# An attention and a convolution layer over eight images: the last 64 gated channels contracted in two row halves, one contraction moved into a parameter chain, and a weight loaded ahead of the last input band

## The chip, the cores and the metric

The kernel runs on one core of a Trainium2 chip. The time is the device time of one execution in microseconds (us). Three executions of the kernel before took 3504.19, 3505.67 and 3510.26 us; the median is 3505.67. In profile lines PE is TensorE (PEld its weight loads), DVE is VectorE, ACT is ScalarE, POOL is GpSimd and SP is SyncE, which mainly issues DMAs. L738 means line 738 of the kernel before.

## The reference

Eight float32 images of 384 channels and 64x64 pixels pass through two residual layers, each behind a group normalisation over 32 groups. The first is linear attention with six heads; the second a patchwise Fourier filter, a depthwise 3x3 convolution and a gated output product. In outline:

```
t = group_norm(x)
q, k, v = Wq t + bq, Wk t + bk, Wv t + bv      # rotary positions on q and k; then elu + 1
x = x + Wfc (q (k^T v) / (q . sum k)) + bfc
t = w_in group_norm(x)                          # 384 -> 384 channels
t = irfft2(rfft2(8x8 patches of t) * fft_filter)
t = depthwise_3x3(t, w_dw)
x1, x2 = t[:, :192], t[:, 192:]
x = x + w_out (gelu(x1) * x2)                   # 192 -> 384 channels
```

The change concerns the last line: the product with w_out contracts over 192 channels, one and a half times the 128 rows of the array.

## The kernel before, in words

An image has 4096 tokens (pixels), worked on in 8 bands of 512; its 384 channels are three tiles of 128 (index m or t). Every matmul is float32, and each one in the code appears as two instructions in the profile. PSUM is used as eight banks of 128x512 that `ps_tile` hands out in turn, so a matmul that takes a bank first waits until the bank's last reader has finished.

For each image b there are two stages. The query stage, `queries` (from L810), projects the queries (`pq`, L525), normalises them and projects the attention output (`pf`, L604), adding it into x. In its first band it also runs the gate of the previous image's last band, and in its third band (L848) it calls `output`, the contraction of that band. Then comes the parameter chain of the second normalisation, `norm_chain(b, 1, ...)` (L922 to L929): group sums and their redistribution as very small matmuls (`ps_m`, `ps_mc`, `ps_v`, `ps_r`) with small DVE steps in between (L289 to L313). For images 0 to 6 the first key projections of the next image fill the chain; for image 7 there is no next image, and nothing fills it.

The layer-1 stage is the loop at L933 to L968, nine steps for eight bands. A step j holds: `expand_filter` (`pi` L622, with ScalarE copies to `ht` L629, and the forward transform `pd` L636 in 64x64 tiles of the array, then the filter on DVE, L644); `back_transform` (`pb` L653, copied by ScalarE into a ring of rows, L660, whose borders GpSimd copies, L669); `first_taps` (L700, ScalarE); key projections of the next image (`pk` L430, bias on DVE into `kc` L433, rotary products L413, L421 and L437, then L337) and their accumulation (`acc` L445); the contraction of band j-2 (`contract`, L738); and, at the end, `depthwise_gate` of band j-1. That gives 7 contractions in a layer-1 stage and one in the next image's query stage. Image 7's own layer-1 stage (L980 to L996) has no next image beside it; it holds all of that image's 8 contractions, and its last two bands take the third channel tile's taps on TensorE.

`depthwise_gate` is 24 tap instructions of DVE (L714; the first of the nine taps is made by ScalarE in `first_taps`), then `gate_taps` (L717 to L723): channels 0 to 127 of x1 go through a gelu in ScalarE (L720) and are multiplied by x2 on DVE (L722); the other 64 channels of x1, on partitions 0 to 63 of the third tile, go through a 64x512 gelu (L721) into partitions 64 to 127 of the second half of `gated`, where they are multiplied by x2 (L723). Partitions 0 to 63 of that second half stay zero (L260), as do the matching rows of `w_out` (L247).

`contract` then needs two matmuls for each output tile, both with 128 rows and N=512; in the second, half of the rows are zeros:

```
for m in range(CT):
    p_ = ps_tile(f"pw_{b}_{j}_{m}")
    for s in range(2):
        nc.tensor.matmul(p_, w_out[:, s, m * P : (m + 1) * P], g[:, s, :], start=(s == 0), stop=(s == 1))
```

DVE adds each tile to x (L744). For image 7's bands 0 to 6 ScalarE copies it to `y` instead (L742), a GpSimd DMA accumulates y into x (L749), and SP sends x out (L751); the last band goes out in three DMAs.

At the start SP's queue loads x's eight bands (the first in three DMAs, L145; the others L147), then the key weight wk (L224). ScalarE's queue loads group masks and the key bias `bk_bc`. DVE computes statistics of each band as it lands (L157). In `layer0_chain` (L754) the group sums of wk (`sum_weight`, `pg_wk` L343) are issued after the fourth step of the parameter chain.

The order of instructions on each engine is fixed when the program is built; at run time an engine takes its own in that order and waits on semaphores.

## Time and profile before

| | |
|---|---|
| median of three runs | 3505.67 us |
| the profiled execution | 3504.77 us, of which the span from first to last instruction is 3503.0 |
| mean granted TensorE clock | 0.994 |
| PE / DVE / ACT / POOL busy | 98% / 83% / 52% / 4% |
| contraction matmuls (L738) | 768 instructions, 343.0 us busy |
| taps on DVE (L714) | 1520 instructions, 1054.8 us |
| x adds on DVE (L744) | 171 instructions, 115.9 us |
| gate products on DVE (L722; L723 of 64x512) | 64, 43.6 us; 62, 42.7 us |
| gelus on ACT (L720; L721 of 64x512) | 39.9 us; 39.0 us |

A group's line names source line, engine, operation, the tile written and those read, shapes and count; then its busy time and the mean of one in ns, the idle time of the engine ahead of it and what ended most of that. Consecutive matmuls overlap: a matmul of N=512 is listed with 596 ns, but from the start of one to that of the next takes about 430. The cost of a stretch of matmuls is therefore read from start to start. In a row of a table of stages come the window, its length, the busy time and count of PE, PEld, DVE, ACT and POOL, the granted clock, the DMA share and GB/s. In a timeline a row is a stretch of alike instructions: start, length, engine, line, operation, tiles, count, and in brackets the idle time ahead of it and its releaser.

### The profile page before, as it was taken

How to read it: one execution, taken by the hardware profiler on the slowest of the kernel's cores; microseconds unless marked ns; L12 is line 12 of the kernel's file. 1: busy time of each engine (PE TensorE's matmuls, PEld its weight loads, DVE VectorE, ACT ScalarE, POOL GpSimd, SP SyncE). 2: the span in 40 equal slices, each digit the busy share in tenths (PEclk: the TensorE clock that was granted, in tenths of full speed). 3: DMA queues.
4: the chain of work that ended last, by engine and by line, in shares of the span. 5: the costliest groups of instructions: out<-in, count | busy, mean ns of one | idle time of the engine just before them, and what ended most of it. 6: DMA issues, size and time to landing. Idle time of an engine off the chain costs nothing.

```text
span 3503.0 us, 38501 instructions
## 1 busy us (share of the span) xinstructions
PE 3438.7 (98%) x14384; PEld 1872.3 (53%) x14384; DVE 2894.7 (83%) x4499; ACT 1805.7 (52%) x3242; POOL 128.3 (4%) x305
## 2 busy tenths in 40 slices
PE   8999999999999999999999999999999999999998
PEld 5545565455554556545565455644555446554454
DVE  7586998868988699886998869987799877998688
ACT  4445563456544565445553555635655354534553
POOL 0000000000000000000000000000000000000011
PEclk9999999999999999999999999999999999999999
DMA  6321233212332122321223212232123211222013
GB/s 214 110 70 52 73 101 113 76 52 73 109 109 84 49 81 90 117 79 46 99 73 129 67 45 100 94 108 67 46 99 116 97 56 34 75 80 88 15 45 90
DMA packets 124641, 290.76 MB, mean 83 GB/s; under 512 B 26101, under 2 KB 36518, under 8 KB 116262
## 3 DMA queue, kind: packets, MB, share of 16 engines
q1 hardware_dynamic: 123110, 282.39, 23.9%
q0 software_dynamic: 1008, 5.51, 0.8%
q8 instruction: 113, 1.85, 0.2%
q14 instruction: 74, 0.61, 0.1%
q10 hardware_dynamic: 336, 0.41, 0.0%
HBM read 232.44 MB, written 50.33 MB: 81 GB/s over the span
## 4 chain that ended last, share of the span: by engine, by line
PE 79%; DVE 12%; issue 4%; ACT 3%; POOL 1%; DMA 1%; ACTq 0%; POOLq 0%
PE pq L525 15%; PE pf L604 15%; PE acc L445 12%; PE pk L430 11%; PE pi L622 8%; DVE dw L714 7%; PE pw L738 7%; PE pb L653 3%; PE pd L636 2%; PE px L396 1%; PE pn L563 1%; DVE kc L437 1%; ACT ring L660 1%; POOL ring L669 1%; DVE x L744 1%
## 5 line engine op out<-in xcount | busy, mean ns | idle before, releaser
L714 DVE SCALAR_TENSOR_TENSOR dw<-ring,w_dw,dw 128x512 f32<-128x512 f32 x1520 | 1054.8, 747 | 118.5 <-ACT dw L700 96.1
L430 PE MATMUL pk<-wk,x 128*128 128x384 f32 x1536 | 542.8, 493 | 0.1
L525 PE MATMUL pq<-x,wq 128*128 128x512 f32 x1152 | 520.2, 599 | 0.7
L604 PE MATMUL pf<-qc,mt 128*128 128x512 f32 x1152 | 513.7, 599 | 0.0
L622 PE MATMUL pi<-w_in,hf 128*128 128x384 f32 x1536 | 509.8, 489 | 2.2 <-ACT hf L330 1.4
L445 PE MATMUL acc<-xk,kc 128*128 128x385 f32 x1488 | 502.4, 490 | 9.0 <-DVE kc L337 9.0
L445 PEld LDWEIGHTS acc<-xk,kc 128*128 128x128 f32 x1488 | 279.9, 190 | 227.1 <-issue 46.5
L622 PEld LDWEIGHTS pi<-w_in,hf 128*128 128x128 f32 x1536 | 290.6, 191 | 200.6 <-issue 5.5
L430 PEld LDWEIGHTS pk<-wk,x 128*128 128x128 f32 x1536 | 279.2, 192 | 177.2 <-issue 21.5
L525 PEld LDWEIGHTS pq<-x,wq 128*128 128x128 f32 x1152 | 212.8, 190 | 252.3 <-issue 234.6
L604 PEld LDWEIGHTS pf<-qc,mt 128*128 128x128 f32 x1152 | 213.4, 190 | 249.6 <-issue 232.5
L738 PE MATMUL pw<-gated,w_out 128*128 128x512 f32 x768 | 343.0, 596 | 0.6 <-DVE gated L722 0.6
L397 ACT COPY xk<-px 128x384 f32<-128x384 f32 x248 | 116.4, 478 | 343.1 <-PE px L396 342.2
L629 ACT COPY ht<-pi 128x384 f32<-128x384 f32 x256 | 121.5, 475 | 234.0 <-PE pi L622 233.4
L608 DVE SCALAR_TENSOR_TENSOR x<-pf,bfc,x 128x512 f32<-128x512 f32 x192 | 141.1, 743 | 107.5 <-PE pf L604 106.8
L738 PEld LDWEIGHTS pw<-gated,w_out 128*128 128x128 f32 x768 | 141.5, 191 | 159.0 <-issue 141.9
L653 PE MATMUL pb<-idft,tf 128*128 128x128 f32 x1536 | 188.9, 278 | 11.6 <-DVE tf L644 11.6
L653 PEld LDWEIGHTS pb<-idft,tf 128*128 128x128 f32 x1536 | 181.7, 193 | 31.2 <-DVE tf L644 20.7
L433 DVE TENSOR_TENSOR kc<-pk,kbias 128x384 f32<-128x384 f32 x256 | 141.1, 551 | 68.3 <-PE pk L430 67.0
L660 ACT COPY ring<-pb 128x512 f32<-128x512 f32 x192 | 109.7, 580 | 158.1 <-PE pb L653 157.4
L335 ACT ACTIVATE qs<-qc 128x1536 f32<-128x1536 f32 x64 | 95.0, 1484 | 170.5 <-DVE qc L554 160.5
L335 ACT ACTIVATE ks<-kc 128x1536 f32<-128x1536 f32 x64 | 95.0, 1485 | 136.1 <-DVE kc L437 124.4
(153 smaller groups left out, 4032.2 us busy)
## 6 DMA issues: line engine op xcount, KB each, us to landing
tq<-in_tq SPq DMA_DIRECT2D x64, 1024.0 KB, 4.8
tk<-in_tk SPq DMA_DIRECT2D x64, 768.0 KB, 4.3
x<-in_x SPq DMA_DIRECT2D x63, 768.0 KB, 4.6
out_dram<-x SPq DMA_DIRECT2D x63, 768.0 KB, 3.3
xs<-in_x SPq DMA_DIRECT2D x56, 768.0 KB, 5.1
x<-y POOLq DMA_DIRECT2D x7, 768.0 KB, 5.7
wk<-in_wk SPq DMA_DIRECT2D x8, 576.0 KB, 4.0
wv<-in_wv SPq DMA_DIRECT2D x8, 576.0 KB, 6.1
```

The costliest lines, as they stand in the source:

```text
L335: nc.scalar.activation(e, x_, AF.Relu, scale=-1.0)
L430: nc.tensor.matmul(pk[:, :C], tokens(t), wks[:, t, :], start=(t == 0), stop=(t == CT - 1))
L433: nc.vector.tensor_add(kc[:, i, :], pk[:, :C], bias)
L445: nc.tensor.matmul(acc[m][:, : C + 1], kf[:, i, m * P : (m + 1) * P], xk[:, i, :], start=(j == 0 and i == 0), stop=(j == NBAND - 1 and i = ...
L525: nc.tensor.matmul(p_, wqs[:, t, m * P : (m + 1) * P], xt[b, j][:, t, :], start=(t == 0), stop=(t == CT - 1),)
L604: nc.tensor.matmul(p_, mt[:, t, m * P : (m + 1) * P], q[:, t, :], start=(t == 0), stop=(t == CT - 1))
L608: nc.vector.scalar_tensor_tensor(xm, p_, bfc[:, m : m + 1], xm, ALU.add, ALU.add)
L622: nc.tensor.matmul(p_[:, :C], h[:, t, i * P : (i + 1) * P], w_in[:, t, :], start=(t == 0), stop=(t == CT - 1),)
L653: nc.tensor.matmul(patches[:, k // 2, k % 2], tf[:, k, m * P : (m + 1) * P], idft.rearrange("p (u n) -> p u n", u=2), start=True, stop=True,)
L660: nc.scalar.copy(t[:, m, 1:9, 1 : W + 1].rearrange("p r (b c) -> p r b c", c=8), p_.rearrange("p (b r c) -> p r b c", b=8, r=8),)
L714: nc.vector.scalar_tensor_tensor(acc[:, m], src, wd, acc[:, m], ALU.mult, ALU.add)
L738: nc.tensor.matmul(p_, w_out[:, s, m * P : (m + 1) * P], g[:, s, :], start=(s == 0), stop=(s == 1))
```

## The change

The contraction becomes a generator, `contraction`. The output is split into two token halves of 256 (h). The products of the first 128 channels come first, for all three output tiles and both halves (N=256). Then the last 64 channels: rows 0 to 63 of the array hold the first 256 tokens, rows 64 to 127 the last 256, as two row tiles of 64x128 with N=256, so that no row holds zeros. Four PSUM banks are held instead of three, by pairs of output tiles (0 and 1; 2) and halves. The gate writes the halves in two 64x256 gelus, one of them to a new tile `gelu2`, and two 64x256 products. The adds become two of 128x(2x256) and two of 128x256, all behind the half products; ScalarE's copies for image 7 likewise, and the last band's output goes in four DMAs.

Image 6's last contraction leaves image 7's query stage and is spread over the steps of image 7's parameter chain. At the start, x's first band is one DMA, wk is loaded ahead of x's last band, `bk_bc` moves from ScalarE's queue to SP's behind that band, and `sum_weight(wk)` is issued ahead of the parameter chain. The last 64 rows of w_out are loaded twice and the two zero fills go.

```diff
--- before.py
+++ after.py
@@ -19,6 +19,7 @@
 N = H * W
 NBAND = 8
 BT = N // NBAND
+HT = BT // 2
 NH = 6
 HD = 64
 NG = 32
@@ -140,11 +141,7 @@
         if b >= nb:
             return
         t = xp.tile([P, CT, BT], F32, tag="x", name=f"x_{b}_{j}")
-        if b == j == 0:
-            for m in range(CT):
-                nc.sync.dma_start(t[:, m], x_in[b][:, m, j * BT : (j + 1) * BT])
-        else:
-            nc.sync.dma_start(t, x_in[b][:, :, j * BT : (j + 1) * BT])
+        nc.sync.dma_start(t, x_in[b][:, :, j * BT : (j + 1) * BT])
         xt[b, j] = t
     stats, moments = {}, {}
@@ -207,7 +204,7 @@
     group_w = {}
-    for j in range(NBAND):
+    for j in range(NBAND - 1):
         load_x(0, j)
     k_runs = ((0, 0, C),)
@@ -239,12 +236,12 @@
     )
     ident = groups[:, 2 * CT * NG :]
     of_group = const_tile([NG, C], "of_group", a["of_group"])
-    bk_bc = const_tile([P, C], "bk_bc", a["bk"].partition_broadcast(P))
     first_wk = load_weight(0, "wk", k_runs)
+    load_x(0, NBAND - 1)
+    bk_bc = const_tile([P, C], "bk_bc", a["bk"].partition_broadcast(P), nc.sync)
     scale = HD ** -0.5
     halves = (slice(0, 64), slice(64, P))
     w_out = const.tile([P, 2, C], F32, tag="w_out", name="w_out")
-    nc.gpsimd.memset(w_out[0:64, 1, :], 0.0)
     kvt_bd = const.tile([P, CT, P], F32, tag="kvt_bd", name="kvt_bd")
@@ -256,8 +253,8 @@
     for i in range(2):
         ring.append(const.tile([P, CT, 10, W + 2], F32, tag=f"ring{i}", name=f"ring{i}"))
-    gated = const.tile([P, 2, BT], F32, tag="gated", name="gated")
-    nc.gpsimd.memset(gated[0:64, 1, :], 0.0)
+    gated = const.tile([P, BT + HT], F32, tag="gated", name="gated")
+    gelu2 = const.tile([P, HT], F32, tag="gelu2", name="gelu2")
     def norm_chain(b, layer, params):
@@ -717,38 +714,65 @@
         g = gated
         af = dw.pop((b, j)).rearrange("p t r w -> p t (r w)")
         last = dw_pe.pop((b, j)) if on_array(b, j) else af[:, 2, :]
-        nc.scalar.activation(g[:, 0, :], af[:, 0, :], AF.Gelu)
-        nc.scalar.activation(g[64:P, 1, :], last[0:64, :], AF.Gelu)
-        nc.vector.tensor_mul(g[:, 0, :], g[:, 0, :], af[:, 1, :])
-        nc.vector.tensor_mul(g[64:P, 1, :], g[64:P, 1, :], last[64:P, :])
+        nc.scalar.activation(g[:, :BT], af[:, 0, :], AF.Gelu)
+        nc.vector.tensor_mul(g[:, :BT], g[:, :BT], af[:, 1, :])
+        for h, gelu in enumerate((gelu2[64:P, :], g[64:P, BT:])):
+            of = slice(h * HT, (h + 1) * HT)
+            nc.scalar.activation(gelu, last[0:64, of], AF.Gelu)
+            nc.vector.tensor_mul(g[halves[h], BT:], gelu, last[64:P, of])
     def depthwise_gate(b, j):
         taps(b, j)
         gate_taps(b, j)
-    def contract(b, j):
-        g = gated
+    def contraction(b, j):
         x_ = xt.pop((b, j))
         adding = b == nb - 1 and j < NBAND - 1
+        pairs = ((0, 2), (2, 3))
+        ps = [[ps_tile(f"pw_{b}_{j}_{m0}_{h}").rearrange("p (m n) -> p m n", m=2) for h in range(2)] for m0, _ in pairs]
+        for (m0, m1), p_ in zip(pairs, ps):
+            for m in range(m0, m1):
+                for h in range(2):
+                    nc.tensor.matmul(
+                        p_[h][:, m - m0, :],
+                        w_out[:, 0, m * P : (m + 1) * P],
+                        gated[:, h * HT : (h + 1) * HT],
+                        start=(m == m0),
+                        stop=False,
+                    )
+            yield
+        for (m0, m1), p_ in zip(pairs, ps):
+            for m in range(m0, m1):
+                for h, half in enumerate(halves):
+                    nc.tensor.matmul(
+                        p_[h][:, m - m0, :],
+                        w_out[half, 1, m * P : (m + 1) * P],
+                        gated[half, BT:],
+                        start=False,
+                        stop=(m == m1 - 1),
+                    )
+            yield
         y = w_tile([P, CT, BT], f"y_{b}_{j}") if adding else None
         to = x_out[b][:, :, j * BT : (j + 1) * BT]
-        for m in range(CT):
-            p_ = ps_tile(f"pw_{b}_{j}_{m}")
-            for s in range(2):
-                nc.tensor.matmul(
-                    p_, w_out[:, s, m * P : (m + 1) * P], g[:, s, :], start=(s == 0), stop=(s == 1)
-                )
-            if adding:
-                nc.scalar.copy(y[:, m, :], p_)
-            else:
-                nc.vector.tensor_add(x_[:, m, :], p_, x_[:, m, :])
-                if b == nb - 1:
-                    nc.sync.dma_start(to[:, m], x_[:, m, :])
+        for (m0, m1), p_ in zip(pairs, ps):
+            for h in range(2):
+                of = (slice(None), slice(m0, m1), slice(h * HT, (h + 1) * HT))
+                if adding:
+                    nc.scalar.copy(y[of], p_[h][:, : m1 - m0, :])
+                else:
+                    nc.vector.tensor_add(x_[of], p_[h][:, : m1 - m0, :], x_[of])
+                    if b == nb - 1:
+                        nc.sync.dma_start(to[of], x_[of])
         if adding:
             nc.gpsimd.dma_start(out=x_, in_=y, accum_op=ALU.add)
         if adding or b < nb - 1:
             nc.sync.dma_start(to, x_)
+    def contract(b, j):
+        run(contraction(b, j))
     def layer0_chain(b, prepared):
@@ -756,10 +780,9 @@
             return
         wk = load_weight(b, "wk", k_runs) if b else first_wk
         params = []
-        for i, _ in enumerate(norm_chain(b, 0, params)):
-            if b == 0 and i == 3:
-                sum_weight(wk, "wk")
-            yield
+        if b == 0:
+            sum_weight(wk, "wk")
+        yield from norm_chain(b, 0, params)
         scale_weight(wk, params)
         yield
         prepared += params, wk, k_bias(b, params)
@@ -845,7 +868,7 @@
                 run(output_)
                 if j < NBAND - 2:
                     next(chain, None)
-            if j == 2:
+            if j == 2 and b < nb - 1:
                 output()
             if j in (4, 5):
                 load_x(b + 1, j - 4)
@@ -885,7 +908,8 @@
     idft = const_tile([P, P], "idft", a["idft"], nc.sync)
     w_dw = const_tile([P, CT, 9], "w_dw", a["w_dw"], nc.sync)
     nc.sync.dma_start(w_out[:, 0, :], a["w_out"][0:P, :])
-    nc.sync.dma_start(w_out[64:P, 1, :], a["w_out"][P : P + 64, :])
+    for half in halves:
+        nc.sync.dma_start(w_out[half, 1, :], a["w_out"][P : P + 64, :])
     bqs = const.tile([P, CT], F32, tag="bqs", name="bqs")
     nc.vector.tensor_scalar_mul(bqs, bq, scale)
@@ -920,14 +944,18 @@
         keys = Keys(b + 1, prepared)
         params = []
         chain, more = norm_chain(b, 1, params), chain_of(keys.project(0), keys.project(1))
-        for steps in (2, 1, 1, 3):
+        last = b == nb - 1
+        if last:
+            more = contraction(b - 1, NBAND - 1) if b else iter(())
+        for steps in (2, 0, 1, 1) if last else (2, 1, 1, 3):
             next(chain)
             for _ in range(steps):
                 next(more, None)
         run(chain)
         ahead = normalised(b, 0, params, (8, 8), "f")
         run(more)
-        if b == nb - 1:
+        if last:
             break
         first_sums = chain_of(keys.accumulate(0), keys.accumulate(1))
         for j in range(NBAND + 1):
```

## The prediction

> **What bounds the kernel now.** I read the page's busy shares first, then a table of stages (window, length, busy us of PE, PEld, DVE, ACT, POOL), because a share over the whole span mixes stages with different limits.
>
> ```profile
> PE 3438.7 (98%) x14384; PEld 1872.3 (53%) x14384; DVE 2894.7 (83%) x4499; ACT 1805.7 (52%) x3242; POOL 128.3 (4%) x305
> ...
> L738 PE MATMUL pw<-gated,w_out 128*128 128x512 f32 x768 | 343.0, 596 | 0.6 <-DVE gated L722 0.6
> ```
> ```profile
> 1871.40:2050.30 178.90, 178.69 (x805) 86.64 (x804) 135.64 (x235) 89.86 (x164) 4.01 (x14) 1.00 0.22 74
> 2050.30:2301.50 251.20, 247.55 (x988) 145.48 (x988) 227.00 (x332) 138.90 (x251) 9.70 (x22) 0.99 0.27 91
> 2186.50:2220.50 34.00, 34.00 (x140) 20.37 (x136) 32.66 (x47) 19.87 (x35) 1.11 (x3) 1.00 0.28 93
> ...
> 3313.00:3323.40 10.40, 3.42 (x26) 3.08 (x26) 3.54 (x20) 4.21 (x8) 0.00 (x0) 0.71 0.00 1
> ```
> The first row is image 4's query stage: PE never idle, DVE busy 76%, so PE's work sets the time. The second is its layer-1 stage: PE 98.5%, DVE 90%. The third is one of that stage's bands: PE 34.0 of 34.0 and DVE 32.7. "PE busy" there doesn't mean that PE alone sets the pace; the timeline of DVE and PE in that band shows a second loop (start, length, engine, line):
>
> ```profile
> 2194.47 2.33 DVE L714 SCALAR_TENSOR_TENSOR dw<-ring,w_dw,dw 128x512 f32<-128x512 f32 x3 [0.82 <-ACT dw L700]
> ...
> 2211.83 8.16 DVE L714 SCALAR_TENSOR_TENSOR dw<-ring,w_dw,dw 128x512 f32<-128x512 f32 x12
> 2219.91 0.55 DVE L433 TENSOR_TENSOR kc<-pk,kbias 128x384 f32<-128x384 f32 x1
> ```
> ```profile
> 2196.89 5.32 PE L738 MATMUL pw<-gated,w_out 128*128 128x512 f32 x12
> 2202.05 7.93 PE L445 MATMUL acc<-xk,kc 128*128 128x385 f32 x24
> 2209.81 7.90 PE L622 MATMUL pi<-w_in,hf 128*128 128x384 f32 x24
> 2217.55 2.10 PE L430 MATMUL pk<-wk,x 128*128 128x384 f32 x6
> ...
> 2219.91 1.52 PE L636 MATMUL pd<-ht,dft 64*64 64x384 f32 x16
> 2221.36 0.91 PE L430 MATMUL pk<-wk,x 128*128 128x384 f32 x2
> ```
> DVE runs from its first tap at 2194.47 to the kc add that ends at 2220.46, with only 0.24 us of idle in between. In both kernels' instruction order the last forward-transform tile (pd_3, L636) waits for exactly that kc add, since it takes its PSUM bank. From there PE must do pd, two pk/px pairs and pb, ACT the ring copy and first product (L660, L700), before DVE's next run starts: 8.0 us (2220.46 to 2228.5, one period of 34.04 on). So DVE's loop is 26.0 + 8.0 = 34.0 us, PE's own sum is 34.0 as well, and the contraction (L738) lies outside DVE's loop.
>
> [...] L636 issues 16 instructions of N=384 in 64x64 tiles between 2219.91 and 2221.36, 1.45 us; 24 unpacked ones of N=384 (L622) take 7.74 us, 322 ns each. Four packed rounds are 1.29, so packing works and entering plus leaving costs about 0.16. [...] The trace shows 3.41 us stretches at half clock, one after the stalls in each of five layer-1 stages, and 10.2 us around the final chain.
>
> **The change, part by part**, summed against the profiled execution (3504.77 us, span 3503.0); the median of the runs, 3505.67, is 0.90 above it.
>
> *Contraction on PE.* Now 12 instructions of N=512: 2196.89 to 2202.05, 5.16 us, 430 ns each. Each product is two instructions. N=256 isn't shown; by proportion with 384 (322) and 512 (430) it is 215 ns. After: 6 whole products, 12 x 0.215 = 2.58; six half products, 12 instructions in 6 concurrent rounds, 1.29; mode switch 0.16, and some 0.1 for the first pair after it: 4.1. Saving 1.05 us (bounds: 0.1 if the two row halves don't overlap, 1.3 if the switch is free).
>
> *Where that counts.* Query stages of images 1 to 6 hold one contraction each (the previous image's last band), PE-bound on both sides; its PSUM waits in the new order are on DVE work finished 2 us or more before. 6 x 1.05 = **-6.3**. Image 7's query stage loses the whole contraction: **-5.2**.
>
> *Layer-1 stages 0 to 6*, 7 contractions each. PE gets to pd_3 1.05 us sooner and waits for the same kc add: the saving becomes a wait. At bands 2 and 3 DVE is already the later one (PE stalls of 1.25, 0.91 and 0.90 us near 2117 and 2148). The eighth step has the same fate: the next stage's first pq, at 2301.52 now, in the new order waits for the first x add, queued on DVE behind the kc product (L437, ended 2301.55 less the 0.6 us add that no longer precedes it): about 2301.6. DVE's added work: three adds of 128x512 become two of 128x(2x256) and two of 128x256, one 64x512 product becomes two 64x256. Start to start an add of 512 takes 0.60 us (2201.22 to 2201.82), one of 384 0.467 (2197.76 to 2198.23): 0.067 of it is fixed, so splitting a 512 in two adds 0.067, for the adds and for the products: +0.13 a band. Some of it falls into the roughly 0.12 us by which each gate product now trails its issue. I take +0.05 x 49 = **+2.5**; bounds -0.12 x 49 = -6 and +0.13 x 49 = +6.4.
>
> *Gelus* (ACT, two of 64x256 for one of 64x512) add nothing: ACT is 55% busy. What they hold up, the gate products, are followed by 12 taps before anything of PE waits. The dropped zero fills were done by 2.1 us in: nothing.
>
> *Final chain* (image 7, L922 on). PE timeline now:
>
> ```profile
> 3316.20 0.32 PE L271 MATMUL ps_m<-mv,groups 128*32 128x1 f32 x6 [3.17 <-DVE mv L202]
> 3316.76 0.82 PE L279 MATMUL ps_mc<-gm,of_group 32*128 32x1 f32 x6 [0.24 <-DVE gm L289]
> 3318.43 0.48 PE L271 MATMUL ps_v<-d,groups 128*32 128x1 f32 x6 [0.84 <-DVE d L296]
> 3320.29 1.44 PE L279 MATMUL ps_r<-rsg,of_group 32*128 32x1 f32 x6 [1.38 <-DVE rsg L308]
> 3323.08 1.65 PE L622 MATMUL pi<-w_in,hf 128*128 128x384 f32 x2 [1.35 <-ACT hf L330]
> ```
> The whole products (2.6) fit into the 3.17; half products behind ps_m and ps_mc delay the next step by about 0.4 and 0.2 with their mode switches; on DVE the four x adds stand between the chain's steps, about 1.2 us of 1.9 uncovered. So +1.8, less what a better-filled PE saves in half clock (now about 2.1 us: pi starts in it and leaves it 4.3 us later). I take half of that: **+0.7**, bounds -2.2 to +2.5.
>
> *Start.* wk's group sums (pg_wk, 27.42, 3.6 us at half clock) now hold ps_r until 30.94 though its operand is ready at 28.9; moved ahead of the chain they free up to 2.0. But x's bands land 1.93 us apart, DVE's statistics follow each landing, and the last band (landed 21.48) now queues on SP behind wk (576 KB, 1.45 us at that rate), while the 192 KB bias leaves the front for behind it (-0.5): the chain starts 1.0 later. x's first band as one DMA lands at 7.9 where the third part does; the next landing at 9.90 covers it. Half clock may outlast the chain[...]. Net **-0.5**, bounds -1.5 and +1.0.
>
> *Layer 1 of image 7.* Its chain is DVE taps; no contraction on it but the last: +0.07 x 8 for the gate products, **+0.5**. The four output DMAs in place of three, each 0.48 us to issue on SP behind the last accumulate, against an accumulate about 1 us sooner: 0, bounds ±0.7.
>
> Sum: -6.3 - 5.2 + 2.5 + 0.7 - 0.5 + 0.5 = -8.3. 3504.77 - 8.3 = 3496.5 beside the profile; with the 0.90 to the median, about **3497**.
>
> **Rivals.**
> - *The saving holds in layer 1 as well.* For it: PE is 98.5% busy there and its own sum equals the period. Against: the DVE run without idle. In full, 49 x 1.05 = -51 and no +2.5: 3444; with half, about 3470.
> - *Slower: DVE's run grows in layer 1.* The four adds now stand together behind L437, after the last product, instead of spread; ACT's turn of the keys behind L437 has 4 taps and the adds as cover (4.5 us against 4.4 needed) instead of 7 taps. If a stall of 0.4 us opens there in each of 49 bands: 3497 + 20 = 3517. It decides from 0.32 us a band on (15.7 / 49). Against: in my ordering the run stays within 0.15.
> - *Nothing left:* half products don't overlap when K=64 spans all columns (the trace shows only 64x64 tiles), so image 7's -5.2 alone remains, against +6.4 of DVE: 3507.
>
> **Chances.** 0.2%, 7 us, is about what a measurement of this kernel can tell from no change: under 3498.7 is faster, above 3512.7 slower. Forecast 0.55 (own range 3489 to 3504; two thirds of it, 0.37, under 3498.7, 0.18 the same); saving in layer 1, partly or in full, 0.25; slower 0.11; nothing left 0.09. Faster 0.62, same 0.27, slower 0.11. The range leaves out the deeper part of the gain (0.09) and the slower case (0.11): 3462 to 3508.
>
> **What would show it.** Right: contraction 4.1 us from pw's first start to the next matmul; query stages 177.9 long; layer-1 stages still 251 with PE idle up by some 5 us each, put down to pd or pq waiting for DVE; the DVE run still 26.0 to 26.2. Wrong: layer-1 stages of 245 or less (DVE's loop wasn't binding), contractions near 5 us (no overlap), DVE idle inside its run behind ACT's keys (the slower case), or more than 13.6 us from image 7's last pf to its first pi (now 3312.01 to 3323.08, 11.1).

## The result, and the profile after

The changed kernel took 3509.07 us (median of 12 runs, 3504.94 to 3514.06), the kernel before 3505.84 beside it (12 runs, 3504.15 to 3510.26). The ratio is 1.0008 with a 95% interval of 1.0000 to 1.0015: a few us slower or equal, not 8 us faster, and outside the stated range of 3462 to 3508. The profiled execution of the changed kernel took 3512.19 us (span 3510.4), 3.1 above its own median.

The page after, its busy shares and three groups of TensorE (line, engine, operation; then busy us, mean ns, idle ahead and what ended it):

```profile
PE 3409.0 (97%) x15152; PEld 1937.9 (55%) x15152; DVE 2908.4 (83%) x4620; ACT 1814.4 (52%) x3313; POOL 131.6 (4%) x303
...
L522 PE MATMUL pq<-x,wq 128*128 128x512 f32 x1152 | 523.7, 602 | 16.0 <-DVE x L765 15.3
...
L738 PE MATMUL pw<-gated,w_out 128*128 128x256 f32 x768 | 181.3, 383 | 6.9 <-DVE tf L641 6.9
```

TensorE has 30 us less to do and finishes 7 us later: it waits 37 us more. Before, the query projection (L525 there) had 0.7 us of idle ahead of it in the whole kernel; now it has 16.0, behind the x adds, and the whole products wait 6.9 us for the filter products. Neither wait was there before.

The table of stages, first of before and then of after (window, length, busy us of PE, PEld, DVE, ACT, POOL, then the granted clock): in each a query stage, the layer-1 stage behind it, image 6's layer-1 stage, and image 7's query stage with its final chain.

```profile
1011.10:1190.00 178.90, 178.72 (x804) 86.65 (x803) 135.65 (x235) 89.89 (x164) 4.00 (x14) 1.00 0.22 74
1190.00:1441.20 251.20, 247.53 (x988) 145.52 (x988) 226.97 (x332) 138.91 (x251) 9.70 (x22) 0.99 0.28 91
2910.50:3158.40 247.90, 245.63 (x988) 145.28 (x988) 224.10 (x324) 116.00 (x176) 9.10 (x22) 1.00 0.19 64
3158.40:3323.10 164.70, 157.63 (x707) 73.58 (x706) 120.75 (x194) 79.40 (x151) 3.40 (x12) 0.98 0.16 55
```
```profile
1015.30:1193.40 178.10, 177.85 (x816) 87.51 (x816) 135.67 (x236) 89.69 (x164) 4.00 (x14) 1.00 0.22 74
1193.40:1445.30 251.90, 244.11 (x1072) 152.39 (x1072) 228.85 (x347) 140.56 (x259) 10.50 (x22) 0.99 0.27 91
1623.40:1877.90 254.50, 245.38 (x1072) 153.03 (x1072) 228.85 (x347) 140.44 (x259) 10.51 (x22) 0.99 0.27 90
1877.90:2057.40 179.50, 179.26 (x816) 88.08 (x816) 135.66 (x236) 89.71 (x164) 4.00 (x14) 0.99 0.22 74
2917.30:3167.90 250.60, 240.81 (x1073) 151.69 (x1073) 226.89 (x338) 117.42 (x185) 10.06 (x22) 1.00 0.19 65
3167.90:3329.50 161.60, 158.00 (x717) 74.54 (x717) 119.20 (x196) 78.68 (x150) 3.80 (x12) 0.99 0.15 52
```

The query stage is 0.9 us shorter, as its contraction is. The layer-1 stage has 3.4 us less of TensorE's work and is 0.7 us longer. The third and fourth rows of after are image 3's layer-1 stage and the query stage behind it, the same work as the first two, 2.6 and 1.4 us longer, with 3.41 us more of half clock (a granted clock of 0.50) in each. In image 3 that is only a half of it, as these lines show:

```profile
1713.12 0.72 ACT L174 ACTIVATE xs<-xs,shift 128x512 f32<-128x512 f32 x1 [2.87 <-DMA xs<-in_x]
...
1719.78 0.42 DVE L722 TENSOR_TENSOR gated<-gelu,dw 64x256 f32<-64x256 f32 x1 [1.36 <-ACT gelu L721]
...
1722.83 0.87 PE L633 MATMUL pd<-ht,dft 64*64 64x384 f32 x6 [2.30 <-DVE kc L430]
```

A load for the next image took 7.92 us to land (6.12 in image 2). ScalarE waited for it, a gelu came after ScalarE's work on it, the gate product waited for that gelu, and TensorE waited 2.30 us for DVE where it waited 1.00 in image 2. Together the two stages lost 4.0 us, enough to explain why this execution is above its median; the other runs were not profiled. From the starts of all stages the 7.4 us between the two spans come as follows (us; a stage's length after minus before):

```
start, up to the first query projection       +2.0
query stages of images 1 to 6                 -3.8   (five at -0.9, one at +0.5)
layer-1 stages of images 0 to 6              +11.2   (+2.3, four at +0.7, image 3 +3.3, image 6 +2.6)
query stage and chain of image 7              -3.0
layer 1 of image 7                            +1.0
```

Within a layer-1 stage the step lengths, from the start of one `pi` block to that of the next, show where (us; images 1, 2, 4 and 5 agree within 0.02):

```
step              0      1      2      3      4      5      6    7 and 8
before          17.99  17.89  21.58  28.38  39.55  34.15  34.04   57.67
after           17.99  17.89  20.80  29.53  38.75  33.51  34.24   59.25
difference        0      0    -0.78  +1.15  -0.80  -0.64  +0.20   +1.58
```

Steps 2, 4 and 5 keep a part of the saving. Step 3 loses some of it, but steps 2 to 4 together are still 0.4 us shorter. The end of the stage loses more than all steps before it kept.

**The end of the stage.** DVE and TensorE before, and then after, from about the last contraction to the first query projection:

```profile
2295.55 5.32 PE L738 MATMUL pw<-gated,w_out 128*128 128x512 f32 x12
...
2297.73 0.68 DVE L744 TENSOR_TENSOR x<-pw,x 128x512 f32<-128x512 f32 x1
...
2299.86 1.75 DVE L437 TENSOR_TENSOR kc<-kc,ks 128x1536 f32<-128x1536 f32 x1
...
2301.52 1.55 PE L525 MATMUL pq<-x,wq 128*128 128x512 f32 x3
2301.53 1.28 DVE L744 TENSOR_TENSOR x<-pw,x 128x512 f32<-128x512 f32 x2
```
```profile
2303.71 0.74 DVE L711 SCALAR_TENSOR_TENSOR dw<-ring,w_dw,dw 128x512 f32<-128x512 f32 x1
2304.37 0.95 DVE L410 TENSOR_TENSOR ks<-kc,tk 128x768 f32<-128x768 f32 x1
2305.24 0.74 DVE L711 SCALAR_TENSOR_TENSOR dw<-ring,w_dw,dw 128x512 f32<-128x512 f32 x1
2305.90 0.95 DVE L418 TENSOR_TENSOR kc<-kc,tk 128x768 f32<-128x768 f32 x1
...
2306.91 1.75 DVE L434 TENSOR_TENSOR kc<-kc,ks 128x1536 f32<-128x1536 f32 x1
2308.57 1.94 DVE L765 TENSOR_TENSOR x<-pw,x 128x512 f32<-128x512 f32 x4
```
```profile
2302.22 2.76 PE L738 MATMUL pw<-gated,w_out 128*128 128x256 f32 x12
2304.91 1.57 PE L749 MATMUL pw<-gated,w_out 64*128 64x256 f32 x12
2306.41 0.80 PE L370 MATMUL pbv<-group_wv,shift 32*1 32x384 f32 x2
2309.31 1.55 PE L522 MATMUL pq<-x,wq 128*128 128x512 f32 x3 [2.10 <-DVE x L765]
```

TensorE is through with the contraction 4.19 us after its start (5.24 before), and stands still for 2.1 us behind one small product (L370): the first query projection starts when the first x add has ended, so by the program's order of banks it takes the one that this add frees, and all four adds come behind the keys' sum (L434). Before, one of three adds stood ahead of that sum, and the projection waited for none of them.

The keys' sum itself starts 249.56 us into the stage, 249.58 before (2306.91 and 2299.86, less the stages' starts at 2057.35 and 2050.28), though an add of 0.60 us no longer stands ahead of it. The projection follows 2.40 us later instead of 1.66, since the add is now behind the sum. That is the stage's 0.7 us.

**What DVE has more to do.** The gate products and the instruction behind them in a full band, before and then after:

```profile
2211.11 0.69 DVE L723 TENSOR_TENSOR gated<-gated,dw 64x512 f32<-64x512 f32 x1
2211.83 8.16 DVE L714 SCALAR_TENSOR_TENSOR dw<-ring,w_dw,dw 128x512 f32<-128x512 f32 x12
```
```profile
2210.49 1.94 DVE L765 TENSOR_TENSOR x<-pw,x 128x512 f32<-128x512 f32 x4
2212.35 2.73 DVE L711 SCALAR_TENSOR_TENSOR dw<-ring,w_dw,dw 128x512 f32<-128x512 f32 x4
...
2219.36 0.42 DVE L722 TENSOR_TENSOR gated<-gelu,dw 64x256 f32<-64x256 f32 x1
2219.82 0.42 DVE L722 TENSOR_TENSOR gated<-gated,dw 64x256 f32<-64x256 f32 x1
2220.27 6.84 DVE L711 SCALAR_TENSOR_TENSOR dw<-ring,w_dw,dw 128x512 f32<-128x512 f32 x10
```

From start to start the one product took 0.72 us and the two halves take 0.46 and 0.45, that is 0.19 more. The four adds take 1.86 us, three of 0.60 took 1.80. Together DVE has 0.25 us more to do in a band.

**Step 3**, the contraction that comes ahead of the back transform:

```profile
2125.08 0.86 PE L633 MATMUL pd<-ht,dft 64*64 64x384 f32 x4 [0.91 <-ACT ht L626]
2125.88 0.70 PE L738 MATMUL pw<-gated,w_out 128*128 128x256 f32 x2
2127.31 2.43 PE L738 MATMUL pw<-gated,w_out 128*128 128x256 f32 x10 [0.74 <-DVE tf L641]
```

The second whole product waits 0.74 us for the first filter product: it writes the other token half, in a second bank, by the program's order one that the forward transform still holds. The old form's three banks were asked for one after the other, each only after two instructions of 430 ns. Another 0.44 us wait stands ahead of `pi` in the same step, for an add of the contraction before.

### The profile page after: what moved, and what is told of

It reads as the page before. It is cut to its first block, busy times and chain, and to the rows that moved or that the text cites. A ratio compares the mean times of both kernels' runs of the same rounds, so it can differ in the third digit from the quotient of the medians.

```text
span 3510.4 us, 40210 instructions
## 1 busy us (share of the span) xinstructions
PE 3409.0 (97%) x15152; PEld 1937.9 (55%) x15152; DVE 2908.4 (83%) x4620; ACT 1814.4 (52%) x3313; POOL 131.6 (4%) x303
## 5 line engine op out<-in xcount | busy, mean ns | idle before, releaser
L442 PE MATMUL acc<-xk,kc 128*128 128x385 f32 x1488 | 507.2, 493 | 11.2 <-DVE kc L334 11.2
L738 PE MATMUL pw<-gated,w_out 128*128 128x256 f32 x768 | 181.3, 383 | 6.9 <-DVE tf L641 6.9
L174 ACT ACTIVATE differences<-x,shift 128x512 f32<-128x512 f32 x168 | 119.9, 714 | 77.0 <-DVE x L605 77.0
```

The source lines that it names most:

```text
L442: nc.tensor.matmul(acc[m][:, : C + 1], kf[:, i, m * P : (m + 1) * P], xk[:, i, :], start=(j == 0 and i == 0), stop=(j == NBAND - 1 and i = ...
L738: nc.tensor.matmul(p_[h][:, m - m0, :], w_out[:, 0, m * P : (m + 1) * P], gated[:, h * HT : (h + 1) * HT], start=(m == m0), stop=False,)
```

## The experiments

Kernels of one group ran on one chip, beside runs of the kernel before (medians 3505.58, 3506.23, 3505.60 and 3506.17 in the four groups; in the second a seventeenth run took 7087 us and is left aside). "Stage" means the length from the profiled execution, images 1, 2, 4 and 5 unless said otherwise.

### The three parts, one at a time

**The half-row contraction alone** (start and final chain as before).

> The kernel before with the half-row contraction alone (gate, banks, adds as in the change; start and final chain as before). Theory A (layer 1 is set by DVE's loop, and the new order of the adds makes it longer): query stages 178.0 each instead of 178.9 (six or seven of them, -6), layer-1 stages 252.0 instead of 251.2 (249.7 to 252 for image 0, 247.9 to 250.5 for image 6), so +8 to +9 there and +1 in image 7's: 3508 to 3510. Rival B (the halves are a gain, and start and final chain lose it): 3497 to 3500.

Measured: 3511.54 (3508.96 to 3519.40), ratio 1.0019 (1.0012 to 1.0027). Query stages 178.0, layer-1 stages 252.0 (image 0 250.5, image 6 251.0). Theory A as to the stages, a little above its total: the halves alone cost 4 to 9 us. The profiled execution was the fastest of its runs; the others scatter upwards by up to 10.

**The start alone** (all four parts of it; two are shown).

```diff
-    for j in range(NBAND):
+    for j in range(NBAND - 1):
         load_x(0, j)
...
-    bk_bc = const_tile([P, C], "bk_bc", a["bk"].partition_broadcast(P))
     first_wk = load_weight(0, "wk", k_runs)
+    load_x(0, NBAND - 1)
+    bk_bc = const_tile([P, C], "bk_bc", a["bk"].partition_broadcast(P), nc.sync)
```

> The kernel before with the changed start alone (x's first band in one DMA, wk ahead of the last band, the key bias on SP, group sums of wk ahead of the chain). Theory A (the first key projection starts 0.9 us sooner, but TensorE's half clock lasts 7 us longer[...]): +2.0 at the first query projection, 3507.5 to 3508. Rival B (the half clock there belongs to the changed contraction's loads or to chance): -1 at the first query projection, 3505.

Measured: 3505.74 (3504.18 to 3508.19), ratio 1.0000 (0.9992 to 1.0008): no difference. Its profiled execution has the +2.2 at the first query projection and a half clock until 37.7 us, but the median does not follow it. Theory A's later start shows in this execution and not in the median, B's earlier one in neither: what one execution shows of the start is not what the runs show. The end of the half clock there moves from profile to profile, with the old start too. Over all profiles taken, first query projection against the end of the half clock (us):

```
start of before:  157.86 (30.1)  158.27 (30.4)  158.28 (30.4)  158.39 (30.8)  159.16 (32.2)  159.41 (32.2)
                  161.69 (39.0)  161.91 (39.3)  162.02 (39.2)  162.43 (39.7)
changed start:    158.34 (34.2)  158.96 (34.9)  159.25 (36.2)  159.58 (36.6)  160.29 (37.6)  160.43 (37.7)
```

At a like end of the half clock, interpolated, the changed start is some 0.8 to 1.7 us sooner, as its first key projection is (31.76 instead of 32.64), but the half clock ends later than in the good half of the old starts, and over the runs it comes out even. In the start of before the group sums ran for 3.6 us inside the chain; no run moved them alone, so whether that sets the end of the half clock was not shown.

**The final chain alone** (contraction in the old form, its matmuls and adds spread over the chain as in the change).

```diff
-            if j == 2:
+            if j == 2 and b < nb - 1:
                 output()
...
-        for steps in (2, 1, 1, 3):
+        last = b == nb - 1
+        if last:
+            more = contraction(b - 1, NBAND - 1)
+        for steps in (2, 0, 1, 1) if last else (2, 1, 1, 3):
```

> The kernel before with image 6's last contraction, in its old form, within the final parameter chain, alone. Theory A (the query stage of image 7 loses 5.2 us, the chain gets about 2 longer, with a phase of the half clock that can give or take 2): 3502 to 3504. Rival B (the contraction's x adds and matmuls lengthen the chain by as much as the query stage gains): 3506.

Measured: 3503.51 (3500.88 to 3507.07), ratio 0.9991 (0.9983 to 0.9999). Image 7's query stage with chain takes 160.8 instead of 164.7: theory A, a gain of 2.1 us by the medians and 3.9 by this stage.

**The changed kernel with the old start.**

> The changed kernel with the start of the kernel before. Theory A: 2.0 less than the changed kernel, 3507. Rival B (start is neutral): 3509. If it comes below 3504, the phase of the half clock after the start also sets what later stages lose.

Measured: 3505.77 (3503.76 to 3510.16), ratio 1.0003 (0.9995 to 1.0011). Inconclusive for the start: 3.3 less than the changed kernel, which ran in another group, though the start alone is worth nothing; set against their own runs of before, the two intervals overlap. The halves' +6.0 and the chain's -2.1 don't add up to this +0.2 either. The clock differs too (mean granted clock of the runs 0.989 to 0.992 with the halves alone, 0.993 to 0.995 with the chain alone, 0.992 to 0.993 here); how much of these us is that and how much is scatter stays open.

### What sets layer 1

**The last contraction of the stage ahead of the last key projection.**

```diff
             else:
                 run(keys.accumulate(j - 2))
+                contract(b, j - 2)
             run(project)
-            if j > 3:
+            if 3 < j < NBAND:
                 contract(b, j - 2)
-                if j < NBAND:
-                    load_x(b + 1, j)
+                load_x(b + 1, j)
```

> The changed kernel with one move: in the ninth step of a layer-1 stage the contraction of band 6 stands ahead of the key projection of band 7, so that its x adds are done long before the next stage's first query projection. Theory A (the 1.6 us that the last steps lose come from that projection waiting for an x add queued behind the keys' sum): the wait of 2.1 us goes, the two last steps take 57.3 to 58.2 instead of 59.26, layer-1 stages 250 to 251 instead of 252, total 3499 to 3503. Rival B (the last steps are longer because DVE has more to do): 252 stays, as another wait takes its place, total 3508.

Measured: 3508.52 (3505.19 to 3511.18), ratio 1.0003 (0.9995 to 1.0012). The last steps took 57.65, as theory A has it, but the query stages took 180.0 instead of 178.0 with TensorE no longer full (178.3 busy): the wait moved into the next stage. Rival B's total, by another way than it gave: putting TensorE's work earlier there gains nothing.

**Less of TensorE's work** (kernel before, with the product of the last 64 channels left out).

```diff
-            for s in range(2):
-                nc.tensor.matmul(
-                    p_, w_out[:, s, m * P : (m + 1) * P], g[:, s, :], start=(s == 0), stop=(s == 1)
-                )
+            nc.tensor.matmul(p_, w_out[:, 0, m * P : (m + 1) * P], g[:, 0, :], start=True, stop=True)
```

> The kernel before with the contraction's second product left out (the last 64 channels are not contracted): 2.58 us of TensorE less a contraction, DVE and ScalarE unchanged. Theory A (layer 1 is set by DVE's loop): query stages 176.3 instead of 178.9, layer-1 stages 248 to 251 instead of 251.2, total 3470 to 3487. Rival B (TensorE sets layer 1, and it was the new order that lost the gain): layer-1 stages 18 shorter, 233, total near 3360.

Measured: 3396.43 (3393.65 to 3396.53), ratio 0.9685 (0.9672 to 0.9699). Its stages:

```profile
1577.60:1815.00 237.40, 228.66 (x946) 137.32 (x947) 222.58 (x330) 138.21 (x250) 9.76 (x22) 0.99 0.28 95
1815.00:1991.30 176.30, 176.10 (x798) 85.33 (x797) 137.27 (x237) 93.04 (x167) 4.01 (x14) 1.00 0.23 77
```

The total lies between the two theories, and A falls in its strict form. The layer-1 stage got 13.8 of the 18.1 us that TensorE saved, with DVE's instructions the same in number and kind. What differs is their order, which is made when the program is built and came out differently (why, no run shows): the first key-bias add now stands before the last taps, and taps fill the time in which DVE waits for the forward transform (the second of the two full steps 32.04 instead of 34.04). So the 26.0 us run that the prediction saw in the trace was a property of the order as much as of DVE's amount.

**Less of DVE's work**, in the kernel before and in the changed one: both leave out the ninth tap of two of the three channel tiles.

```diff
-            for k in range(1, 9):
+            for k in range(1, 8 if m < 2 else 9):
```

> The kernel before with the ninth tap left out for two of three channel tiles: 1.33 us of DVE less a band, TensorE unchanged. Theory A (both loops are 34.0 long, so TensorE takes over at once): layer-1 stages 0 to 6 at 249 to 250.5 instead of 251.2, image 7's 10 shorter, total 3481 to 3490. Rival B (DVE alone sets layer 1): 242, total 3430.

> The changed kernel with the same taps left out (ninth tap of two channel tiles). Theory A: with DVE's loop 1.3 shorter a band TensorE's saving shows, layer-1 stages at 244 to 247 instead of 252, total 3455 to 3475, that is 15 to 30 below the kernel before with those taps left out. Rival B (the halves save nothing that layer 1 could use): no better than the kernel before with those taps left out.

Measured: 3479.57 (3478.51 to 3480.87) and 3462.22 (3458.32 to 3466.41), ratios 0.9924 (0.9910 to 0.9939) and 0.9875 (0.9861 to 0.9889). Layer-1 stages 247.0 with the old contraction, where the full steps stay at 34.15 and 34.04: there TensorE's own sum holds. With the halves the same steps take 33.28 and 33.18, and the stages 245.1 to 247.8. With less of DVE in the way the whole change is worth 17 us. Little of that is layer 1: where no half clock fell its stages are 1.9 us shorter, of some 7 us that TensorE saves in each. Theory A holds for the second; for the first it is nearer than B, but stages and total came out 2 us below its ranges.

**DVE's order alone** (theory C, formed after the run with one product).

```diff
-            nc.vector.tensor_add(kc[:, i, :], pk[:, :C], bias)
+            added = nc.vector.tensor_add(kc[:, i, :], pk[:, :C], bias)
+            if i == 0:
+                first_add[b, j] = added
...
-                nc.vector.scalar_tensor_tensor(acc[:, m], src, wd, acc[:, m], ALU.mult, ALU.add)
+                tap = nc.vector.scalar_tensor_tensor(acc[:, m], src, wd, acc[:, m], ALU.mult, ALU.add)
+                if 3 <= j < NBAND - 1 and 8 * m + k > 12 and (b + 1, j) in first_add:
+                    tc.add_manual_dep(tap.ins, first_add[b + 1, j].ins.name, mybir.DependencyInfo(mybir.DependencyClass.NoSync, mybir.DependencyReason.DATA), reason="order")
```

> The changed kernel with nothing but DVE's order changed: in bands 3 to 6 of a layer-1 stage the taps from the thirteenth on are issued behind the first key-bias add (kc) of the same step, which so comes two taps earlier, and taps fill DVE's wait behind it. Theory C (what ate the saving is the place of that add in DVE's order, since the last forward-transform tile waits for it, and not the amount of DVE's work): the two steps of 33.5 and 34.25 go to 32.9 to 33.3, layer-1 stages 247 to 250 instead of 252, total 3475 to 3495. Rival D (DVE has too much work): 252 stays, total 3509.

> The kernel before with the same constraint on DVE's order. Theory C: TensorE's own sum holds the full bands at 34.0, only the stalls of the middle steps can go, layer-1 stages 249.5 to 251.2, total 3495 to 3506; the halves are then worth 10 or more against this one. Rival D (the order is worth the same whatever the contraction): as much less than the kernel before as the changed kernel gains by it.

Measured: the changed kernel with it 3501.49 (3496.43 to 3505.47), ratio to the kernel before 0.9985 (0.9979 to 0.9992); the kernel before with it 3499.01 (3496.63 to 3505.79), ratio 0.9983 (0.9976 to 0.9990). In the changed kernel the two full steps went from 33.51 and 34.24 to 33.28 and 33.17 with no instruction less: theory C as to the steps. In the kernel before they stayed at 34.15 and 34.04, held by TensorE, and its gain came from the last steps (57.03 instead of 57.67). But the total is above theory C's, the layer-1 stages with it, and the halves are not ahead of the kernel before. The stages of the changed kernel with the order:

```profile
1189.50:1439.90 250.40, 243.80 (x1073) 153.07 (x1073) 228.01 (x348) 140.46 (x259) 8.86 (x22) 0.99 0.27 92
1439.90:1619.60 179.70, 179.49 (x815) 88.03 (x815) 135.52 (x235) 89.62 (x164) 4.02 (x14) 0.99 0.21 73
```

The query stage takes 179.7 instead of 178.0, as 3.41 us of half clock begins 0.5 to 0.7 us into each one (580.3, 1010.4, 1440.5 us and so on). The three largest waits of TensorE in one of its layer-1 stages:

```profile
PE pq L526 <- DVE x L771: 2.2, 1, 2.2
PE acc L446 <- DVE kc L334: 1.8, 2, 0.9
PE pd L637 <- ACT ht L630: 0.9, 1, 0.9
```

### Where the halves pay

**The halves for band 7 only** (the contraction in the query stage), image 6's in the final chain. Gelu and product of the halves use the free part of the old `gated` tile, whose zero rows are filled again behind each contraction.

```diff
+    def in_halves(b, j):
+        return b < nb - 1 and j == NBAND - 1
...
         def output(b=b):
-            contract(b, NBAND - 1)
+            run(contraction(b, NBAND - 1))
```

> The kernel before with half-row contraction for each image's last band only (the one in the next query stage, where TensorE alone sets the time), image 6's in the final parameter chain; layer 1 and the start as before. If the loss lies in layer 1: query stages 178.0 instead of 178.9, layer-1 stages 251.2 as before, image 7's query stage and chain 3 to 5 less: 3496 to 3500. Rival (the halves lose as much in the query stage by waits and half clock): 3503 to 3506.

Measured: 3491.13 (3490.51 to 3495.81), ratio 0.9961 (0.9949 to 0.9974): 14 us less. Query stages 178.0, layer-1 stages 251.3 or, where no half clock fell into step 4, 249.7; image 7's query stage 160.7 and its layer 1 177.8 instead of 179.9. By stages that is 5.2 + 3.9 + 2.1, the last for a stretch of half clock that is gone there. The total is below the range that was expected. Without halves in layer 1 the loss is gone, so it lay there. What the stages leave of the 14 us is not shown by stage: the profiled run, of 3495.81, had a mean granted clock of 0.995, the other four, of 3490.51 to 3491.45, had 0.996 or 0.997.

**The halves everywhere in images 0 to 6 but for band 6**, with DVE's order constrained as above and the start of before. Against the last run, next to the constraint:

```diff
-        return b < nb - 1 and j == NBAND - 1
+        return b < nb - 1 and j != NBAND - 2
```

> Half-row contraction for every band of images 0 to 6 but band 6, whose contraction stands at the end of a layer-1 stage and keeps the old form with three banks; DVE's order constrained as in the run with the changed kernel; start of the kernel before, image 7's layer 1 in the old form. Theory C with a second term (the first query projection's wait for an x add behind the keys' sum costs its 2.1 us, and the half clock that follows costs the query stage another 1.7): against the changed kernel with that order, the last two steps 57 instead of 58.3, query stages 178.0 instead of 179.7, layer-1 stages 249 to 250, total 3485 to 3492. Rival E (the half clock at the query stage's start comes from the earlier stalls): 179.7 stays, total 3497.

Measured: **3478.35** (3476.66 to 3481.68), ratio 0.9919 (0.9905 to 0.9932), the fastest complete version. Its stages and TensorE's four largest waits in one layer-1 stage:

```profile
1182.90:1431.40 248.50, 243.34 (x1060) 150.96 (x1060) 226.71 (x344) 139.91 (x258) 10.01 (x23) 0.99 0.27 92
1431.40:1609.40 178.00, 177.81 (x816) 87.45 (x815) 136.33 (x237) 89.90 (x164) 4.27 (x15) 1.00 0.23 75
```
```profile
PE acc L449 <- DVE kc L337: 1.8, 2, 0.9
PE pd L640 <- DVE kc L435: 1.0, 1, 1.0
PE pd L640 <- ACT ht L633: 0.9, 1, 0.9
PE pw L779 <- DVE tf L648: 0.7, 1, 0.7
```

The wait of the query projection is gone, the last steps take 57.10 instead of 58.33, and the query stages are at 178.0 at full clock. Theory C with its second term; the total is even below its range. Against the changed kernel with the same order, 23 us come from one contraction of eight in its old form (image 7's layer 1, old form too, was 0.1 longer). The stage end accounts for 1.2 us a stage of that, some 9 in all. Most of the rest is half clock that the changed kernel with the constrained order had and this run has not: 1.7 us in each query stage, and 1.1 in step 3 of five layer-1 stages (mean granted clock of the runs 0.987 to 0.990 there, 0.992 to 0.995 here). The waits of step 3 stay (0.7).

**The halves for bands 3, 4, 5 and 7 only.**

> As the last, but half-row contraction only for bands 3, 4, 5 (steps 5 to 7 of layer 1, whose order now leaves TensorE the pace) and 7 (query stage); bands 0, 1, 2 and 6 in the old form. Theory C: full bands at 33.2, 0.85 less each than 34.04; no new stalls in steps 2 to 4: layer-1 stages 247.5 to 249, query stages 178.0, total 3470 to 3484. Rival E: half clock takes the gain back, layer-1 stages 250 and over, total 3488 or more.

Measured: 3481.65 (3476.96 to 3483.14), ratio 0.9924 (0.9911 to 0.9936). Full steps 33.28 and 33.17 as expected, no stall added in steps 2 to 4, layer-1 stages 247.4 to 249.1. It can't be told from the last one. Step 3 is back at 28.37 us here, but steps 2 to 4 take 89.5 us together, against 89.1 with the halves in them: what step 3 loses is less than what its neighbours keep.

**The sum of the parts without halves in layer 1** (band 7, chain, order, changed start).

> The kernel before with half-row contraction for band 7 only, image 6's in the final chain, DVE's order constrained and the changed start. Sum of the single runs: 14 (query stages and chain) and 6 (order) less than the kernel before, the start 0 to 1: 3484 to 3488. If the start's gain (1.2 us at equal clock) is real beyond the phase of the half clock, nearer 3484.

Measured: 3485.76 (3484.28 to 3488.01), ratio 0.9938 (0.9925 to 0.9952): the sum of the single runs. The start's part stays too small to be seen.

## Why the prediction was wrong

**The contraction** was right: 4.1 us forecast, 4.19 measured, from 5.24. The row halves do run together: 12 instructions in 1.49 us (2206.45 to 2207.94 in step 5's band), the two of a pair 0.006 us apart, against 2.69 us for 12 whole ones. Whole products follow each other at 0.216 us and pairs at 0.209, but it is 0.31 us from the last whole one to the first pair, 0.31 to the second and 0.31 from the last pair to the next matmul; that is what the forecast had as the switch.

**The query stages** were right in kind, -0.9 each instead of -1.05; one lost its gain to half clock, so -3.8 in this execution for -6.3.

**Layer 1, +2.5 forecast, +11.2 measured, is the step that failed.** Its main claim held in the trace: from the first tap to the end of the key-bias add DVE runs for 26.24 us in a full band (2201.34 to 2227.58; before 25.99), and the last forward-transform tile waits for that add (12.0 us over the kernel, 6.5 before). Two of its terms were mis-sized, and one was left out:

- DVE's added work, "+0.05 x 49". It is 0.25 us a band, almost twice even the bound of 0.13. I had let a part of it fall into the 0.12 us by which a gate product of 512 takes longer than an add of 512 from start to start (0.72 against 0.60). But each of the two half products costs 0.45 us from start to start, where an add of 256 takes 0.33 in the same profile, so those 0.12 us are paid twice.
- "About 2301.6" for the first query projection at the end of a stage, that is no loss. I let the keys' sum move up by the 0.6 us of the add that no longer stands ahead of it. It didn't move (249.56 us into the stage, 249.58 before): over seven bands DVE's added work is 1.7 us, more than that add, and only 1.1 us of it went into DVE's idle time (24.2 us before that point, 23.1 now). With the first add behind the sum the projection waits 2.1 us, and the stage is 0.7 us longer where I had counted 0.36. The +1.58 in the last steps is more than this, because there TensorE also gives back the 0.9 us by which it was ahead.
- Half clock was priced at the start and in the final chain only. The trace had shown that it follows TensorE's stalls in layer 1 (1.81 us of idle in the 3.41 us ahead of it, in each of five images); the change adds stalls, and 65 us of the execution are at half clock now (41 before). By estimate from the stages' lengths and from half of TensorE's busy time in these stretches, image 3's layer 1 lost about 1.3 us that way (another 1.3 by the late load), the query stage behind it 1.4, image 7's query stage 1.6, and image 0's layer 1 about 1.6, as the same stretch had not fallen into it before. That is some 6 of the 15.7 us between the forecast and this execution.

Seven stages at 0.72 make 5.0 of the 11.2 us, half clock and the late load in images 0 and 3 make 4.2, and image 6, whose end is 2.95 us longer, the remaining 1.9. Why that end loses more than the others stays open. The wait at the stage's end is shown by its going: with the order constrained the last steps take 57.03 without halves, 58.33 with them and 57.10 with band 6 in the old form. DVE's added work is read from the trace; no run took it away alone. The waits of step 3 look like a loss and are none on the whole, as the run with bands 3, 4, 5 and 7 shows.

**What the argument rested on was also too strong.** I took the order of the trace as given, a loop of 34.0 us that no shorter contraction can touch. It is true of the changed program only because its built order still places that add behind the same taps. In the run with one product the same instructions of DVE fit into 32.0 us, and those of the changed kernel, with the order constrained, into 33.2. The rival that I gave 0.25, that layer 1 could keep the saving, came true in a part in those runs, not in this program; the slower rival (0.11) named the adds behind the keys' sum, but priced a stall behind ScalarE's part in each band, where the loss was one wait at each stage's end.

**The final chain and image 7's query stage**: -4.5 forecast, -3.0 measured, within the bounds. From the last attention output to the first `pi` it is 0.6 us longer, for +0.7; without the 3.41 us of half clock at that stage's start (1.6 lost) the sum would be about -4.6. **The start**: -0.5 forecast, +2.0 in the execution, 0 by its own runs. One term was wrong: x's last band landed at 21.44 us (21.48 before), not 1 us later, and the first band had landed at 6.26 us instead of 7.93; so the chain was not delayed. In this execution the half clock ended at 37.6 us instead of 30.4 and took more than that gave. **Image 7's layer 1**: +0.5 forecast, +1.0.

What stays open: whether the changed kernel with the old start is really 3 us below that with the new one, and which image loses to half clock in which run.

## What to carry to other kernels

When an engine's work is cut inside a loop that two engines share, price from the trace what the cut adds to the other engine, for each kind of instruction that is split. Then look up in the new program's order what the next user of each buffer waits for, at stage ends above all: a result that leaves its bank behind a longer instruction than before can cost more there than the cut gains (here a wait of 2.1 us at a stage's end, for 1.05 us less of contraction). Use the cheaper form where its engine alone sets the time (here the query stages, 0.9 us shorter each), and in shared stages only where its buffers come free in time. And if the order is made at build time, a run with one constraint on it tells whether an engine is short of time or only badly ordered.

## What the runs showed of the hardware

- In the profiles of before and after, the granted clock was 1.0 or 0.5 and nothing else. Half clock (0.5) came in stretches of 3.41 us or multiples of it (up to 13.65), but for the one at the end, which reaches past the last instruction. In the changed kernel they start at 433.5, 863.6, 1293.7, 1723.8, 1877.4 and 2157.3 us and so on, all of them whole multiples of 3.413 us apart (within 0.001), though its stages differ in length.
- A TensorE that was 98% busy still lost clock: the kernel before was at half clock for 41 us. From 60 us on, in the kernel before, each of the eight stretches of that grid at full clock with 1.81 us or more of idle TensorE in it was followed by half clock, and none with 1.41 or less. In the changed kernel the five with 2.13 us or more were, none with 1.46 or less was, and of those from 1.54 to 1.94 seven were and eight were not. How a wait lies in the grid differs too: a wait of 2.1 to 2.2 us at a stage's end was followed by half clock in every image of the changed kernel with the constrained order, but only in two of seven of the changed kernel itself (images 4 and 7). In its image 5, 1.87 of the 2.10 us fell into one stretch, and no half clock followed.
- In the kernel before a pair of stages takes 430.12 us, and 126 stretches of 3.413 are 430.08. So the stall in each of five images falls at almost the same place of the grid (1.81 us of it in one stretch each time), and each of the five gets its half clock (859.9, 1290.0, 1720.0, 2150.1 and 2580.2 us). With the halves for band 7 only, which makes each pair 0.9 us shorter, two of these five images have no half clock.
- The same program differs by some 5 us from run to run: the kernel before has runs near 3504 and runs near 3510, and little between them (30 of 42 up to 3506.05, 12 from 3509.06). The mean granted clock parts them in the same way: 0.994 or 0.995 in the 30, 0.993 in the 12. Which stretches of the 12 were at half clock is not shown.
